# Rows of zeros for a small projection, and another order of Winograd products, in a four-layer network on one core

## The chip, the cores and the metric

The kernel runs on one core of one Trainium2 chip. The metric is the device time of one execution in microseconds, as the median over several executions. The profile comes from one further execution.

The engines are named as the profile names them: PE is the matrix engine (PEld its weight loads), DVE the vector engine, ACT the scalar engine with its activation functions, POOL the general-purpose engine, SP the engine that issues most of the DMAs. [...]

## The reference, cut to what matters

The input is a batch of three images of 256 channels and 48 x 48 points in float32. Four layers follow one another, each added to its input after a normalisation over groups of 8 channels:

```python
x = x + layer0(_gn(x))                                   # attention over 3 images, 1x1 convolutions
x = x + layer1(_gn(x), routing_ws, weight)               # 3x3 convolution, weights mixed per image
x = x + layer2(_gn(x), weight, bias)                     # plain 3x3 convolution with bias
x = x + layer3(_gn(x), ...)                              # state space layer (selective scan)

# layer 1: each image has its own weights, a mix of eight experts
routing = sigmoid(x.mean(axis=(2, 3)) @ routing_ws)
ws = einsum('ne,eoihw->noihw', routing, weight)

# layer 3, the part around the dt projection (DT_RANK = 16, D_STATE = 16, D_INNER = 512)
x_dbl = einsum('bld,ed->ble', u, x_proj_w)               # 48 values for each point: dt, B, C
dt = softplus(einsum('blr,dr->bld', x_dbl[..., :16], dt_proj_w) + dt_proj_b)
h = h * exp(dt * A) + dt * B * u                         # the scan, over the 2304 points of an image
```

## The kernel before, in words

**Stages.** Layer 0 runs until about 1500 us and takes nearly half of the time. The two convolutions run from about 1498 to 1995 us, the state space layer from about 1990 us to the end. Images are always taken in the order 2, 1, 0.

**The convolution stage.** A unit is one layer and one image: first image 2, 1 and 0 of layer 1, then the same three of layer 2. A unit has two halves of 24 rows (`h`), a half two output tiles of 128 channels (`m`). The 3 x 3 convolution is done in a Winograd form along the row: four points at a time are made from six products. `input_transform` (L316) normalises half an image into a padded tile `xpad` on ACT and makes the six input parts `vt[:, 0]` to `vt[:, 5]` of it with twelve DVE operations (L345 to L356). `output` (L642) calls `products` (L1630) once for each of the six taps: 6 float32 matmuls into a bank of PSUM, from a pool of five banks. Each matmul stands as two records in the profile. Taps 1 and 3 belong together, and 4 and 5: ACT copies the second of a pair to SBUF (L1650), DVE makes the sum and the difference (L1652, L1654), and these are put onto the four points of the image tile (L1659 to L1662). The outer taps 0 and 2 each go onto one point only, with a single DVE operation (L1664).

The order in `output` before the change is 1, 3, then 4, 5, then 0, 2:

```python
for i, j in ((1, 3), (4, 5)):
    pa, pb = products(u, vt, m, i), products(u, vt, m, j)
```

The input transform of a half is asked for one half ahead (`ahead = transformed(n + 1)`), so it stands in the program in front of the output tiles of the half before.

**The mixed weights.** During units 0 and 1 the weights of the next image are made (`mixed`, L265): 8 experts x 6 pieces of 384 KB come in by DMA on SP's queue (`part_of_kernel`, L251) into six buffers `wconv`. A piece is scaled on ACT for the first expert (L294) and added on DVE for the others (L296). With `shared=True` one piece of six is multiplied on PE instead (L282) and copied back by ACT (L290). After the last expert `kernel_transform` (L254) makes the six taps from the three kernel columns, for each half of the input channels six DVE operations: tap 4 and tap 5 (L259, L260), then tap 3 (L262) and, last, tap 1 (L263), which overwrites the middle column. Taps 0 and 2 are the outer columns as they are mixed. Thirteen steps of this are put behind each output tile. The plain weights of layer 2 are loaded and transformed during unit 2 (`plain`, L302).

The weights of image 2 and the input transform of the first half (`first_v`) are made at the end of layer 0. There the order on every engine is as written (`keep_order`, L2128); in the convolution stage it is left to the framework that builds the program, which takes what it reckons to be ready, earlier places in the program first.

**The state space stage.** It runs over 18 chunks (`todo`: three images, six chunks of 384 points each). A chunk has 8 steps of 8 scans (L1949) on DVE; their decays come from ACT (L1941) and their sums go through PE (L1971). The order is written out by hand in `plan` (L1432) and kept on all engines. In between, `project_u` (L1296) makes 96 rows: dt in rows 0 to 15, B in rows 32 to 47, C in rows 64 to 79, and zeros in the rows between. `take_dbc` (L1304) copies them into `dbc`, of 96 rows, and adds a column of the identity matrix, so that row 16 is all ones. `project_dt` (L1323) multiplies `dtsb`, which holds the dt projection's weights in rows 0 to 15 and its bias in row 16, by the first 17 rows of `dbc`; it is called twice a chunk, for two output tiles each (L1326). `keep_busy` (L1374) adds matmuls whose results nobody reads.

`dtsb` is a part of a block (L1138 to L1143) and is loaded once by `w3_loads` (L1153).

Of the kernel before, what the change touches and what calls it, by code (L numbers as in the profile page):

```python
# [12 lines left out]
ALU = mybir.AluOpType  # L13
# [3 lines left out]
P = 128  # L17
# [18 lines left out]
DI = 4  # L36
DS = 16
DTR = 16
# [46 lines left out]
def net(  # L85
# [230 lines left out]
    def input_transform(b, h, sc, sh):  # L316

        rows = HR + 2
        size = rows * PW
        t = pad.tile([P, 4, CT * size + 2], F32, name="xpad")  # L320

        nc.gpsimd.memset(t[:, :, 0 : CT * size + 1 : PW], 0.0)  # L322
        at = (0 if h == 0 else HR + 1) * PW
        for ct in range(CT):
            nc.gpsimd.memset(t[:, :, ct * size + at : ct * size + at + PW], 0.0)
        lo = 1 if h == 0 else 0
        first = h * HR - 1 + lo
        for ct in range(CT):
            src = xs[b][:, ct, :].rearrange("p (j r c) -> p j r c", j=4, c=TW)
            dst = t[:, :, ct * size : (ct + 1) * size].rearrange("p j (r c) -> p j r c", c=PW)  # L330
            nc.scalar.activation(
                dst[:, :, lo : lo + HR + 1, 1:], src[:, :, first : first + HR + 1, :],
                AF.Identity, bias=sh[:, ct : ct + 1], scale=sc[:, ct : ct + 1],
            )

        def column(j, at):
            return t[:, j, at : at + CT * size].rearrange("p (r c) -> p r c", c=PW)[:, :, :TW]

        d = [column(j, at) for j, at in ((3, 0), (0, 1), (1, 1), (2, 1), (3, 1), (0, 2))]
        vt = vp.tile([P, 6, CT, (HR + 2) * TW], F32, name="vt")  # L340
        o = [vt[:, i].rearrange("p t (r c) -> p (t r) c", c=TW) for i in range(6)]
        c = pad.tile([P, CT * rows, TW], F32, name="wc")
        e = pad.tile([P, CT * rows, TW], F32, name="we")
        tt, stt = nc.vector.tensor_tensor, nc.vector.scalar_tensor_tensor
        stt(c, d[2], -4.0, d[4], ALU.mult, ALU.add)  # L345
        stt(e, d[1], -4.0, d[3], ALU.mult, ALU.add)
        tt(o[1], c, e, ALU.add)
        tt(o[3], c, e, ALU.subtract)
        tt(c, d[4], d[2], ALU.subtract)
        tt(e, d[3], d[1], ALU.subtract)  # L350
        stt(o[4], e, 2.0, c, ALU.mult, ALU.add)
        stt(o[5], e, -2.0, c, ALU.mult, ALU.add)
        tt(o[0], d[0], d[2], ALU.subtract)
        stt(o[0], o[0], 4.0, c, ALU.mult, ALU.add)
        tt(o[2], d[5], d[3], ALU.subtract)
        stt(o[2], e, -4.0, o[2], ALU.mult, ALU.add)  # L356
        return vt

    def routing(b, psum, tag, stats):
# [23 lines left out]
    with ExitStack() as l0:  # L383
# [667 lines left out]
        i = NB - 1  # L1051
# [82 lines left out]
    def w3_rooms():  # L1134

        block = upools[0].tile([P, 6, 3, CT, 256], F32, name="u")
        block = block.rearrange("p a b c d -> p (a b c d)")
        w3v.update(divide(  # L1138
            block, ("w3sb", P, (NW3,)), ("winx", P, (CT, DI * P)), ("taps", P, (DI, DCONV, P)), ("convc", P, (DI * DCONV,)),
            ("amat", P, (DI * DS,)), ("rep", P, (4, 32)), ("less", P, (2, P)), ("zero", P, (8,)),  # L1140
            ("xn0", P, (CT, XH)), ("xn1", P, (CT, XH)), ("xi", P, (3, XH)),
            ("dtsb", DTR + 1, (DI * P,)),
        ))  # L1143
        rooms["xn"] = [w3v["xn0"], w3v["xn1"]]
        pieces = [wst.tile([P, 3 * 256], F32, name="wconv") for _ in range(6)]
        halves = [t.rearrange("p (t n) -> p t n", t=2) for t in pieces]
        for name, got in zip(("xg", "sq", "ot"), (halves[:2], halves[2:3], halves[3:5])):
            rooms[name] = got
        rooms["dbc"] = [halves[5][:96, j, :] for j in range(2)]
# [173 lines left out]
    def project_dt(k, m0):  # L1323
        for j in range(2):
            m = m0 + j
            nc.tensor.matmul(  # L1326
                bank[j], w3v["dtsb"][:, m * P : (m + 1) * P], k.dbc[: DTR + 1, :],
                start=True, stop=True,
            )

# [293 lines left out]
    with ExitStack() as l1:  # L1624
# [5 lines left out]
        def products(u, vt, m, i):  # L1630
            pc = ps.tile([P, 512], F32, tag="c", name="ps_c")
            for ct in range(CT):
                for dy in range(3):
                    nc.tensor.matmul(  # L1634
                        pc[:, :HN], u[:, i, dy, ct, m * P : (m + 1) * P],
                        vt[:, i, ct, dy * TW : dy * TW + HN],
                        start=ct == 0 and dy == 0, stop=ct == CT - 1 and dy == 2,
                    )
            between()
            return pc[:, :HN]  # L1640

        def output(b, h, m, u, vt, bias):

            xj = xs[b][:, m, :].rearrange("p (j n) -> p j n", j=4)[:, :, h * HN : (h + 1) * HN]
            tt, stt = nc.vector.tensor_tensor, nc.vector.scalar_tensor_tensor
            sums = []
            for i, j in ((1, 3), (4, 5)):
                pa, pb = products(u, vt, m, i), products(u, vt, m, j)
                cb = tmp.tile([P, HN], F32, name="cb")
                nc.scalar.copy(cb, pb)  # L1650
                add = tmp.tile([P, HN], F32, name=f"add{i}")
                tt(add, pa, cb, ALU.add)  # L1652
                sub = tmp.tile([P, HN], F32, name=f"sub{i}")
                tt(sub, pa, cb, ALU.subtract)  # L1654
                sums += [add, sub]
            p, q, r, s = sums
            for k, (minus, more, f) in enumerate(((p, r, 1.0), (q, s, 2.0), (p, r, 4.0), (q, s, 8.0))):
                if bias is None:
                    tt(xj[:, k], xj[:, k], minus, ALU.subtract)  # L1659
                else:  # L1660
                    stt(xj[:, k], xj[:, k], bias[:, m : m + 1], minus, ALU.add, ALU.subtract)
                stt(xj[:, k], more, f, xj[:, k], ALU.mult, ALU.add)  # L1662
            for i, k, f in ((0, 0, 1.5), (2, 3, 6.0)):
                stt(xj[:, k], products(u, vt, m, i), f, xj[:, k], ALU.mult, ALU.add)  # L1664


        units = [(layer, b) for layer in range(2) for b in ORDER]
# [506 lines left out]
def _layout(i):  # L2174
    l0 = {k[len("L0_conv_"):]: np.asarray(a) for k, a in i.items() if k.startswith("L0_conv_")}
    l3 = {k[len("L3_conv_"):]: np.asarray(a) for k, a in i.items() if k.startswith("L3_conv_")}
    cols = {k: _columns(l0[k]) for k, _ in VEC_WIDTHS if k in l0}
    cols["l2_bias"] = _columns(i["L2_conv_bias"])
    cols["norm_w"], cols["norm_b"] = _columns(l3["norm_w"]), _columns(l3["norm_b"])
    cols["conv_b"] = _columns(l3["conv_b"])  # L2180
    cols["D"] = _columns(l3["D_param"])

    cols["A_log"] = (
        l3["A_log"].reshape(DI, 4, 32, 4, 4).transpose(4, 2, 0, 3, 1).reshape(P, DI * DS)
    )
    vecs = np.concatenate([cols[k] for k, _ in VEC_WIDTHS], 1)

    w0 = {
        "cv1": _rows(l0["cv1_w"].T),
        "qkv": np.concatenate([_rows(a.T) for a in l0["qkv_w"]], 1),  # L2190
        "f1": np.concatenate([_rows(a.T) for a in l0["f1_w"]], 1),
        "f2": np.concatenate([_rows(a.T) for a in l0["f2_w"]], 1),
        "cv2": _rows(l0["cv2_w"].T),
    }

    xp = np.zeros((DI * P, 3, 32), np.float32)
    xp[:, :, :DS] = l3["x_proj_w"].T.reshape(DI * P, 3, DS)
    w3 = {
        "in": _rows(l3["in_proj_w"][DI * P :].T),
        "x": _rows(xp.reshape(DI * P, 96)),  # L2200
        "out": _rows(l3["out_proj_w"].T),
    }
    return {
        "x": np.asarray(i["x"]).reshape(B, CT * P, HN * 2, 4).swapaxes(2, 3).reshape(B, CT * P, N),
        "vecs": vecs,
        "w0": np.concatenate([w0[k] for k, _ in W0_WIDTHS], 1),

        "projw": l0["proj_w"].reshape(NB, P, HD, HEADS).transpose(0, 3, 2, 1).reshape(NB, P, P),
        "qkvb": l0["qkv_b"],
        "rw": np.asarray(i["L1_conv_routing_ws"]),  # L2210

        "we": np.asarray(i["L1_conv_weight"]).transpose(0, 2, 4, 3, 1).reshape(EXPERTS, 256, TAPS * 256),
        "w2": np.asarray(i["L2_conv_weight"]).transpose(1, 3, 2, 0).reshape(256, TAPS * 256),
        "w3": np.concatenate([w3[k] for k, _ in W3_WIDTHS], 1),
        "w3x": l3["in_proj_w"][: DI * P].T,
        "convw": l3["conv_w"].reshape(DI, P, DCONV).transpose(1, 0, 2).reshape(P, -1),
        "dtw": np.concatenate([l3["dt_proj_w"].T, l3["dt_proj_b"][None]]),
    }


# [17 lines left out]
```

## Time and profile before

| | |
|---|---|
| median of 3 runs | 3303.44 us (3302.32 to 3303.94) |
| the profiled execution | 3306.9 us, of which span 3305.1 us |
| mean granted PE clock | 0.983 of full speed |
| convolution stage | about 1498 to 1995 us |
| state space stage | about 1990 to 3305 us |

The span runs from the first to the last instruction of the profiled execution. In the lines of a timeline or of the chain, the first number is the time since the start of the span in us, the second a length in us; "x4" counts instructions, "17*128" gives the rows and columns of the array that a matmul uses, and a bracket the idle time before it and what ended it. In lines of waits, the three numbers are us in total, how many, and the longest.

### The profile page before, as it was taken

To read this page: it belongs to the slowest core of one execution; us is meant where nothing else is said; L and a number is where in the kernel's file an instruction comes from. 1 tells how busy PE (TensorE), PEld (TensorE's weight loads), DVE (VectorE), ACT (ScalarE), POOL (GpSimd) and SP (SyncE) were. 2 spreads that over 40 slices of the span, in tenths; PEclk is the share of its full clock that TensorE was granted. 3 is DMA by queue.
4 is the path that set the end of the run, shared out by engine and by line. 5 is a ranking of instruction groups with operands and counts; after the bars stand their busy time and mean duration, and the time that the engine had idled before them with its cause. 6 is when DMAs were issued, how large, how long until landed. Compare 5 with 4: busy or idle time off the path is not lost.

```text
span 3305.1 us, 54212 instructions
## 1 busy us (share of the span) xinstructions
PE 3140.9 (95%) x20918; PEld 1557.1 (47%) x20918; DVE 2867.9 (87%) x3225; ACT 2393.1 (72%) x3675; POOL 1338.7 (41%) x457
## 2 busy tenths in 40 slices
PE   7999999999999999998999998999999999999996
PEld 4334343363343434556677774444444444444442
DVE  3799989967988999389985449999999999999998
ACT  2688888848888888332223458888888888888885
POOL 0000000000000000120000008999999999999998
PEclk9999999999999999999999999999999999999998
DMA  4000000010000000484621025555555555555552
GB/s 168 32 8 10 7 10 6 8 48 5 8 7 8 8 7 9 153 313 165 222 80 42 34 75 132 139 129 128 136 130 142 140 138 130 130 134 137 141 132 69
DMA packets 182657, 290.98 MB, mean 88 GB/s; under 512 B 34850, under 2 KB 148962, under 8 KB 180467
## 3 DMA queue, kind: packets, MB, share of 16 engines
q1 hardware_dynamic: 169426, 268.53, 30.1%
q10 hardware_dynamic: 12960, 18.88, 1.7%
q8 instruction: 166, 2.72, 0.3%
q14 instruction: 105, 0.85, 0.1%
HBM read 236.24 MB, written 50.64 MB: 87 GB/s over the span
## 4 chain that ended last, share of the span: by engine, by line
PE 55%; DVE 28%; ACT 8%; issue 5%; DMA 2%; POOL 1%; SPq 0%; DVEq 0%; ACTq 0%; POOLq 0%
DVE hs L1949 19%; PE ps_s L640 16%; PE acc L653 15%; PE ps_c L1634 8%; DVE hs L1896 3%; ACT ps_da L1941 2%; PE ps_s L1035 2%; PE ps_y L464 2%; DVE u L296 2%; PE ps_m L667 2%; PE ps_m L713 1%; PE acc L531 1%; PE ps_g L1229 1%; PE ps_s L520 1%; DMA wconv<-in_we 1%
## 5 line engine op out<-in xcount | busy, mean ns | idle before, releaser
L644 ACT ACTIVATE pt<-ps_s 128x1024 f32<-128x1024 f32 x972 | 942.4, 1022 | 154.7 <-PE ps_s L640 142.2
L1949 DVE TENSOR_TENSOR_SCAN hs<-ps_da,hs 128x385 f32<-128x385 f32 x1152 | 1002.6, 936 | 5.6 <-ACT ps_da L1941 4.5
L859 DVE TENSOR_TENSOR part<-part,pt 128x2048 f32<-128x2048 f32 x396 | 906.7, 2290 | 41.2 <-ACT pt L644 18.4
L1941 ACT ACTIVATE ps_da<-dtr,u 128x384 f32<-128x384 f32 x1136 | 642.0, 580 | 116.2 <-DVE hs L1949 105.5
L164 POOL TENSOR_TENSOR rstd<-ve,mhalf 128x2 f32<-128x2 f32 (+1 forms) x25 | 16.0, 642 | 1440.6 <-DVE ve L162 1440.6
L640 PE MATMUL ps_s<-q,kt 32*128 32x512 f32 (+1 forms) x4320 | 576.4, 592 | 0.1
L653 PE MATMUL acc<-pt,vt 128*32 128x512 f32 (+1 forms) x4320 | 520.9, 561 | 0.2
L1634 PE MATMUL ps_c<-vt,u 128*128 128x288 f32 x1728 | 431.9, 410 | 17.6 <-DVE u L263 9.0
L1957 POOL TENSOR_TENSOR hc<-hs,x 128x3072 f32<-128x3072 f32 x72 | 405.3, 5629 | 11.2 <-DVE hs L1949 6.7
L1957 POOL TENSOR_TENSOR hc<-hs,bc 128x3072 f32<-128x3072 f32 x71 | 400.2, 5636 | 9.8 <-POOL hs L1915 3.9
L1634 PEld LDWEIGHTS ps_c<-vt,u 128*128 128x128 f32 x1728 | 330.0, 192 | 114.3 <-DVE u L263 9.7
L640 PEld LDWEIGHTS ps_s<-q,kt 32*128 32x128 f32 x4320 | 195.2, 183 | 199.1 <-issue 120.2
L653 PEld LDWEIGHTS acc<-pt,vt 128*32 128x32 f32 x4320 | 94.4, 108 | 353.4 <-issue 326.7
L1971 PE MATMUL ps_y<-hc,u 128*32 128x384 f32 x2304 | 226.9, 514 | 2.9 <-POOL hc L1957 2.9
L1915 POOL TENSOR_TENSOR hs<-dtur,bc 128x1536 f32<-128x1536 f32 x72 | 209.8, 2913 | 0.0
L1280 PE MATMUL ps_g<-u 128*128 128x384 f32 x576 | 193.6, 488 | 11.6 <-ACT u L1276 11.6
L1915 POOL TENSOR_TENSOR hs<-dtur,x 128x1536 f32<-128x1536 f32 x70 | 203.5, 2907 | 0.0
L1280 PEld LDWEIGHTS ps_g<-u 128*128 128x128 f32 x576 | 107.5, 189 | 94.2 <-ACT u L1276 22.5
L1971 PEld LDWEIGHTS ps_y<-hc,u 128*32 128x32 f32 x2304 | 62.2, 112 | 144.0 <-issue 128.7
L1650 ACT COPY cb<-ps_c 128x288 f32<-128x288 f32 x48 | 19.2, 399 | 150.7 <-PE ps_c L1634 141.5
L322 POOL MEMSET xpad<- 128x212 f32 x12 | 5.7, 475 | 291.6 <-ACT xpad L1685 221.5
L1399 PE MATMUL ps_g<-u 128*128 128x384 f32 x288 | 106.6, 503 | 13.1 <-ACT sz L1407 7.7
(295 smaller groups left out, 4169.8 us busy)
## 6 DMA issues: line engine op xcount, KB each, us to landing
wconv<-in_we SPq DMA_DIRECT2D x144, 384.0 KB, 4.6
dtr<-dtd SPq DMA_DIRECT2D x284, 192.0 KB, 3.7
dtur<-dtud SPq DMA_DIRECT2D x284, 96.0 KB, 4.2
wconv<-xd SPq DMA_DIRECT2D x36, 384.0 KB, 4.0
x<-bcd SPq DMA_DIRECT2D x72, 192.0 KB, 4.9
dtd<-x SPq DMA_DIRECT2D x36, 384.0 KB, 3.0
bc<-bcd SPq DMA_DIRECT2D x72, 192.0 KB, 5.0
dtuq<-dtud SPq DMA_DIRECT2D x284, 48.0 KB, 2.0
```

Source lines behind the costliest of these rows:

```text
L640: nc.tensor.matmul(s[:, j, cols], kt[r, mt * P : (mt + 1) * P], q[r, :n], start=True, stop=True,)
L644: nc.scalar.activation(p[:, h0 : h0 + 2, :], s, AF.Exp)
L653: nc.tensor.matmul(acc[h * HD : (h + 1) * HD, :n], vt[:, mt, g * P + h * HD : g * P + (h + 1) * HD], p[:, h, cols], start=mt == 0, stop=mt ...
L859: ): nc.vector.tensor_tensor(part, first, p, ALU.add)
L1280: nc.tensor.matmul(bank[m % 2], w3v["taps"][:, m, tap, :], w3v["xi"][:, m % 3, tap : tap + CH], start=tap == 0, stop=tap == DCONV - 1,)
L1399: nc.tensor.matmul(bank[j], w("in", ct * 512 + m * P, P), k.xn[:, ct, DCONV - 1 :], start=ct == 0, stop=ct == CT - 1,)
L1634: nc.tensor.matmul(pc[:, :HN], u[:, i, dy, ct, m * P : (m + 1) * P], vt[:, i, ct, dy * TW : dy * TW + HN], start=ct == 0 and dy == 0, stop ...
L1915: nc.gpsimd.tensor_tensor(states(s)[:, :, 2:4, 1:], chunks[at].rows[m][1].unsqueeze(1).broadcast_to([P, 2, 2, CH]), b_rows(s, 0, 2), ALU.mult,
L1941: nc.scalar.activation(slots[n % 3][:, 1 : CH + 1], chunks[at].rows[m][0][:, q, :], AF.Exp, scale=amat[:, col : col + 1],)
L1949: nc.vector.tensor_tensor_scan(b, slots[(8 * s + part) % 3][:, : CH + 1], b, 0.0, ALU.mult, ALU.add)
L1957: nc.gpsimd.tensor_tensor(hc, tiles[s][:, :, :, 1:], cb.broadcast_to([P, 2, 4, CH]), ALU.mult)
L1971: nc.tensor.matmul(k.y_ps[32 * q : 32 * q + 32, :CH], fold, hc[:, g, q, :], start=False, stop=g == 1 and q in ends,)
```

## The change

Two edits are made together.

1. `dtsb` gets 96 rows in place of 17. The host appends 79 rows of zeros to the weights, and `project_dt` multiplies by all of `dbc`. The result is the same sum with 79 more terms of zero.
2. In the first output tile (`m == 0`) of the first half (`h == 0`) of each image, `output` takes the outer taps first: 0, 2, then the pair 4, 5, then the pair 1, 3. Their accumulations (L1664) are put first as well (`ends`). `input_transform` makes its parts in the same order where `h == 0`: parts 0 and 2, then 4 and 5, then 1 and 3. All other output tiles and halves stay in the old order (in the second halves the parts come as 1, 3, 4, 5, 0, 2, as before).

```diff
         ...
+        def odd():
+            stt(c, d[2], -4.0, d[4], ALU.mult, ALU.add)
+            stt(e, d[1], -4.0, d[3], ALU.mult, ALU.add)
+            tt(o[1], c, e, ALU.add)
+            tt(o[3], c, e, ALU.subtract)
+
+        def outer():
+            tt(o[0], d[0], d[2], ALU.subtract)
+            stt(o[0], o[0], 4.0, c, ALU.mult, ALU.add)
+            tt(o[2], d[5], d[3], ALU.subtract)
+            stt(o[2], e, -4.0, o[2], ALU.mult, ALU.add)
+
         ...
-        stt(c, d[2], -4.0, d[4], ALU.mult, ALU.add)
-        stt(e, d[1], -4.0, d[3], ALU.mult, ALU.add)
-        tt(o[1], c, e, ALU.add)
-        tt(o[3], c, e, ALU.subtract)
+        if h:
+            odd()
         tt(c, d[4], d[2], ALU.subtract)
         tt(e, d[3], d[1], ALU.subtract)
+        if not h:
+            outer()
         stt(o[4], e, 2.0, c, ALU.mult, ALU.add)
         stt(o[5], e, -2.0, c, ALU.mult, ALU.add)
-        tt(o[0], d[0], d[2], ALU.subtract)
-        stt(o[0], o[0], 4.0, c, ALU.mult, ALU.add)
-        tt(o[2], d[5], d[3], ALU.subtract)
-        stt(o[2], e, -4.0, o[2], ALU.mult, ALU.add)
+        if h:
+            outer()
+        else:
+            odd()
         return vt
         ...
-            ("dtsb", DTR + 1, (DI * P,)),
+            ("dtsb", 96, (DI * P,)),
         ...
-                bank[j], w3v["dtsb"][:, m * P : (m + 1) * P], k.dbc[: DTR + 1, :],
+                bank[j], w3v["dtsb"][:, m * P : (m + 1) * P], k.dbc,
         ...
+            def ends():
+                for i, k, f in ((0, 0, 1.5), (2, 3, 6.0)):
+                    stt(xj[:, k], products(u, vt, m, i), f, xj[:, k], ALU.mult, ALU.add)
+
+            first = h == 0 and m == 0
+            if first:
+                ends()
             sums = []
-            for i, j in ((1, 3), (4, 5)):
+            for i, j in ((4, 5), (1, 3)) if first else ((1, 3), (4, 5)):
                 pa, pb = products(u, vt, m, i), products(u, vt, m, j)
         ...
-            p, q, r, s = sums
+            p, q, r, s = sums[2:] + sums[:2] if first else sums
         ...
-            for i, k, f in ((0, 0, 1.5), (2, 3, 6.0)):
-                stt(xj[:, k], products(u, vt, m, i), f, xj[:, k], ALU.mult, ALU.add)
+            if not first:
+                ends()
         ...
-        "dtw": np.concatenate([l3["dt_proj_w"].T, l3["dt_proj_b"][None]]),
+        "dtw": np.concatenate(
+            [l3["dt_proj_w"].T, l3["dt_proj_b"][None], np.zeros((95 - DTR, DI * P), np.float32)]
+        ),
```

## The prediction

> **What bounds the kernel now.** I read the page first (shares, granted clock), then the chain of waits in order of time, then the stretches, waits and timelines of the two places that the edits touch.
>
> ```profile
> PE 3140.9 (95%) x20918; PEld 1557.1 (47%) x20918; DVE 2867.9 (87%) x3225; ACT 2393.1 (72%) x3675; POOL 1338.7 (41%) x457
> ```
>
> Nearly everything is busy, so an average says nothing: each edit is priced where it lies. The dt projection (L1326) is in the last stage, a loop over 18 chunks whose clockwork is the scan on DVE. The chain shows the same five scans once a chunk:
>
> ```profile
> 2072.89 4.33 DVE hs L1949 x5
> ...
> 2144.86 4.33 DVE hs L1949 x5
> ...
> 2217.73 4.33 DVE hs L1949 x5
> ...
> 2290.58 4.33 DVE hs L1949 x5
> ...
> 2362.56 4.33 DVE hs L1949 x5
> ```
>
> The distances are 71.97, 72.87, 72.85 and 71.98 us. Two chunks of the four are 0.89 us longer, with the same instructions. The PE timeline of the first long one says why; its last line is the same spot in a short chunk:
>
> ```profile
> 2192.51 1.55 PE L1326 MATMUL ps_g<-wconv,u 17*128 17x384 f32 x4 [0.89 <-ACT x L1389]
> 2193.99 0.91 PE L1964 MATMUL ps_y<-x,diag 128*128 128x384 f32 x2
> 2194.83 2.47 PE L1971 MATMUL ps_y<-hc,u 128*32 128x384 f32 x16
> 2197.23 2.23 PE L1355 MATMUL ps_g<-dtu,ident 128*128 128x384 f32 x4
> ...
> 2340.57 1.50 PE L1971 MATMUL ps_y<-hc,u 128*32 128x384 f32 x16
> ```
>
> The same 16 matmuls take 2.47 us instead of 1.50. The stretches of L1326 (columns: length, PE busy and count, PEld busy and count, granted clock, DMA) show a halved clock for one stretch of 3.41 us:
>
> ```profile
> 2191.80:2195.21 3.41, 1.55 (x4) 0.66 (x4) 1.00 0.68 200
> 2195.21:2198.63 3.42, 0.00 (x0) 0.00 (x0) 0.50 0.67 175
> ...
> 2335.16:2338.57 3.41, 0.32 (x1) 0.29 (x2) 1.00 1.09 212
> 2338.57:2341.99 3.42, 1.23 (x4) 0.37 (x2) 1.00 1.02 292
> ```
>
> The clock drops after a stretch that holds all four 17-row matmuls, and stays after one that holds one of them. The other long chunks repeat it (half clock from 2266.9, 2628.7, 2700.4, 3062.2 and 3133.9): six of them.
>
> The second place is the convolution stage, where the mixed weights of the next image are made on DVE (L296, then L258 to L263) while PE multiplies. Stretches of its first two units (PE, PEld, DVE, ACT, POOL busy, granted clock), then PE's waits and DVE's:
>
> ```profile
> 1498.10:1584.60 86.50, 85.08 (x332) 62.89 (x332) 82.65 (x147) 19.96 (x32) 2.59 (x7) 0.98 0.54 189
> 1584.60:1591.80 7.20, 0.01 (x1) 0.01 (x1) 7.17 (x10) 7.20 (x11) 0.69 (x3) 0.71 0.51 198
> 1591.80:1684.80 93.00, 91.15 (x352) 68.39 (x352) 84.94 (x138) 23.75 (x36) 2.09 (x7) 0.97 0.63 212
> ...
> 1686.00:1758.00 72.00, 72.00 (x299) 56.53 (x300) 52.22 (x113) 19.80 (x26) 2.19 (x8) 1.00 0.07 26
> ```
>
> ```profile
> PE ps_c L1634 <- DVE u L263: 9.0, 2, 7.2
> ```
>
> ```profile
> DVE u L296 <- DMA wconv<-in_we: 6.7, 8, 1.2
> DVE wconv L258 <- ACT u L290: 2.3, 1, 2.3
> DVE add L1652 <- ACT cb L1650: 1.1, 1, 1.1
> ```
>
> PE waits 7.2 us at the change of image, for the last operation of the weight transform (L263 makes tap 1, which is multiplied first). But DVE never rests there (7.17 of 7.20), and from 1498 to 1685 it is idle for 11.9 us alone (the lengths less the DVE column). DVE bounds these two units; from 1686 on PE does (72.00 of 72.00).
>
> **Part 1, zero rows.** No instruction is added or removed. 36 calls of two matmuls (144 records of L1326) read 96 rows in place of 17. Their price is the nearest row's: L1355, 128 rows and the same 384 columns, takes 486 ns against 481, its weight load 190 against 184. That is at most 144 x 5 ns = 0.7 us, in gaps that PE has (0.89 us ahead of L1326): 0. The load of `dtsb` (L1153) grows from 34 to 192 KB; it stays one issue (0.34 us) on SP's queue, and the 512 KB load behind it took 7.0 us to land. First use is at 1954.7, 205 us after the issue at 1749.7: 0. If that cover went, it would cost some 2 us.
>
> The gain is the clock. [...] in the stretch 2191.80 to 2195.21 PE was busy for 2.70 us and lost the clock, in 2335.16 to 2338.57 for 1.93 us and kept it. So what is counted is not busy time. [...] I side with the trace: six drops x 0.89 = 5.3 us off. Bounds: 0 if zeros do not count, 6.2 if another execution meets seven drops.
>
> **Part 2, order of the products.** No instruction is added or removed either; six of the 24 output tiles take products 0, 2, 4, 5, 1, 3 in place of 1, 3, 4, 5, 0, 2, and six input transforms are made in that order. No DMA is moved. Four places:
>
> 1. First unit. PE starts at 1498.09, after the third operation of the input transform. Product 0 needs the fourth, 0.72 us later; half of that is lost, as the clock is halved there until 1502.3: +0.4 (0 to +0.7).
> 2. Change to the second image. Product 0 needs mixed weights only (done at 1583.7), so the 7.2 us wait goes, and the half clock behind it. But L263 is only no longer late for PE; DVE still has it, and an input transform of 8.6 us, ahead of its first use of a product. DVE was free at 1606.10 and started L1652 at 1607.16: -1.1, all that DVE can give back.
> 3. The weight pieces have six buffers; those that PE multiplies (L282) are held until PE comes to them (1612.35), and behind them SP's queue stops. DVE then waits 2.0 us for pieces between 1614.9 and 1622.5, and 2.2 more at 1658 to 1662. PE comes some 7 us sooner: -1.5 (0 to -4.1), most of the first group.
> 4. Change to the third image. PE waits 1.85 and 1.10 us, and starts the second output tile at 1696.22, 0.12 us after L1654 gave a PSUM bank free (1696.10). Product 0 is released by one operation, not two: -0.35. If its accumulation lands in DVE's hole of 2.35 us before L258, PE runs through from 1674.9: six products of 2.91 us end at 1692.4, -3.5 after a short wait for L290. I take -2.0; the order on DVE is not written by hand here, so either can come.
>
> Sum +0.4 - 1.1 - 1.5 - 2.0 = -4.2 us (+0.7 to -8.7). In the three units behind, PE never waits, so nothing is won or lost and the lead passes to the last stage: the chain goes through PE's L1634 and L1326 until 1969.
>
> **The sum.** -5.3 - 4.2 = -9.5. The profiled execution took 3306.9 us (span 3305.1 and 1.8 around it): 3297.4. It stands 3.5 above the median of the runs, 3303.4, which gives 3293.9.
>
> **The rivals.**
> - *Only the clock pays.* DVE has no slack, so PE's 7.2 us lead is eaten at the next PSUM bank. For: DVE's 84.94 of 93.00. Against: L1652 and L296 do wait for what PE does late. -5.0: 3298.4.
> - *The padding does nothing*, [...] because zeros do not count. Then -4.2 alone: 3299.2. [...]
> - *Slower: the two accumulations of products 0 and 2 (L1664) are queued on DVE ahead of the weight transform (L258 to L263).* They wait for PE, which ends product 2 near 1590.1, while DVE could work from 1583.6: 6.5 us per change of image, 13 for two. With 5.3 won it ends near 3311. It decides if such a wait passes some 4 us per change. Against: those operations come earlier in the program than L1664, and the order in the trace keeps that.
>
> **How the numbers follow.** Both parts work: 0.68, only the clock 0.17, the padding does nothing 0.08, slower 0.07. About 6.6 us (0.2%) is what a measurement of this kernel can tell from no change. Both parts together pass it unless part 2 gives under 1.3 (one in ten of these cases counts as same); the two rivals below it mostly do not. Faster 0.67, same 0.26, slower 0.07. Range: from 5.3 + 8.7 with a little more clock (3288.5) to the clock alone with the first unit's loss, and the padding alone (3300).
>
> **What would show it.** After: chunk distances all near 71.95, granted clock 1.00 from 2035 on but for the last 90 us, L1326 as 96*128. No wait of L1634 for L263 near 1584; PE's first L1634 of the second unit some 7 us sooner, but DVE's L1652 about 1 us; fewer waits of L296. I am wrong if the clock still halves after L1326, or if DVE waits on PE at L1664 ahead of L258.

## The result and the profile after

| | before | after |
| --- | --- | --- |
| median of six runs each | 3303.69 us (3299.53 to 3304.06) | 3289.18 us (3286.98 to 3290.58) |
| ratio of after to before, 95% interval | | 0.9957 [0.9947, 0.9968] |
| profiled execution, its span | 3306.9, 3305.1 us | 3289.2, 3287.5 us |
| mean granted clock of TensorE | 0.983 | 0.989 |

The change saves 14.5 us by the medians, 0.43%. The forecast was 9.5 (3293.9 for the median); the result lies inside its range of 3288.5 to 3300, near the low end.

In the profiled executions the spans differ by 17.6 us. I cut each span at four places that both traces share: the end of layer 0's last matmul, the last product of the convolutions (of layer 2; L1634 before, L1646 after), the first scan of chunk 0 and the first scan of chunk 17.

| stretch (us) | before | after | difference |
| --- | --- | --- | --- |
| span's start to layer 0's last matmul | 1490.66 | 1487.64 | -3.02 |
| from there to the convolutions' last product | 504.63 | 495.10 | -9.53 |
| chunk 0's first scan to chunk 17's | 1230.32 | 1224.77 | -5.55 |
| the rest (the two joints and the last chunk) | 79.47 | 79.99 | +0.52 |

The first row is not the change's: layer 0 runs the same code, and over the fourteen kernels traced for this study (twelve experiments, before and after) its end lies anywhere from 1481.87 to 1490.66. The profiled execution of before sits at the late end of that. The second row belongs to the order of products (8.9 of its 9.5 us lie within layer 1, 258.5 to 249.6) and the third to the zero rows: 15.1 together, beside 14.5 by the medians.

**The scan stage.** The chain of waits of after, in order of time (start, length, what), shows the same eight matmuls once a chunk:

```profile
2043.89 2.86 PE ps_g L1241 x8
...
2115.86 2.86 PE ps_g L1241 x8
...
2187.81 2.86 PE ps_g L1241 x8
...
2259.77 2.86 PE ps_g L1241 x8
...
2331.72 2.86 PE ps_g L1241 x8
```

The distances are 71.97, 71.95, 71.96 and 71.95 us; the 72.87 of before is gone. The six stretches at half clock between 2040 and 3200 us have become none. These are the stretches from 2040 to 3200 us of before and of after (length; busy time and count of PE, PEld, DVE, ACT, POOL; granted clock; DMA share; GB/s):

```profile
2040.00:3200.00 1160.00, 1095.54 (x5180) 547.85 (x5180) 1146.68 (x1365) 1016.91 (x2021) 1139.63 (x324) 0.99 0.56 135
2040.00:3200.00 1160.00, 1086.74 (x5188) 548.69 (x5186) 1151.24 (x1373) 1019.17 (x2026) 1145.05 (x326) 1.00 0.56 136
```

The records of L1338 (L1326 before; nanoseconds, lowest, median and highest) show that the rows cost next to nothing on PE, 486 ns against 481:

```profile
L1338 PE MATMUL ps_g<-wconv,u x144: 483/486/592, 1942.8 to 3188.2; 96*128 96x384 f32 x144
```

**Layer 1, where weights are mixed beside the products.** First the stretches from each image's first product to the next image's, for the three images of layer 1, of after and then of before (columns as above):

```profile
1495.95:1583.22 87.27, 84.94 (x330) 63.26 (x331) 81.37 (x146) 19.42 (x30) 2.58 (x7) 0.97 0.53 184
1583.22:1664.60 81.38, 79.91 (x322) 60.24 (x320) 79.69 (x134) 24.54 (x38) 2.08 (x7) 1.00 0.66 229
1664.60:1737.08 72.48, 71.97 (x297) 55.92 (x296) 61.37 (x115) 19.97 (x27) 2.08 (x7) 1.00 0.11 36
```

```profile
1498.09:1591.79 93.70, 85.10 (x333) 62.91 (x333) 89.83 (x157) 27.15 (x42) 3.28 (x10) 0.96 0.54 190
1591.79:1677.28 85.49, 83.64 (x322) 62.80 (x322) 79.77 (x132) 16.41 (x26) 1.39 (x4) 0.96 0.64 215
1677.28:1749.04 71.76, 70.65 (x292) 55.17 (x293) 54.52 (x106) 19.23 (x27) 2.10 (x7) 1.00 0.06 19
```

Compare the DVE columns. The same work is cut elsewhere. When the second image's first product starts, DVE of after has done 8.5 us less (81.37 against 89.83). In the second image it does as much as before in 4.1 us less, because its idle time falls from 5.7 us to 1.7. In the third image it does 6.9 us more (61.37 against 54.52). There it had 17 us to spare, so the debt is paid where DVE limits nothing.

The timeline of PE at the change to the second image, before and then after (start, length, operation, idle time before it in brackets):

```profile
1577.72 3.56 PE L1634 MATMUL ps_c<-vt,u 128*128 128x288 f32 x14
1581.12 2.99 PE L282 MATMUL ps_g<-wconv,each 128*128 128x384 f32 x8
1584.20 0.38 PE L186 MATMUL ps_gm<-mv,gmat 128*128 128x2 f32 x2
1591.79 8.60 PE L1634 MATMUL ps_c<-vt,u 128*128 128x288 f32 x22 [7.20 <-DVE u L263]
```

```profile
1576.76 4.04 PE L1646 MATMUL ps_c<-vt,u 128*128 128x288 f32 x16
1580.64 2.74 PE L282 MATMUL ps_g<-wconv,each 128*128 128x384 f32 x8
1583.22 9.14 PE L1646 MATMUL ps_c<-vt,u 128*128 128x288 f32 x37
```

From the start of the first image's last product to the second image's first PE took 13.6 us before (1578.21 to 1591.79) and 5.5 after (1577.73 to 1583.22). In before, a half clock from 1587.6 to 1597.9 then stretched the first product from 2.91 us to 5.92. In after the clock stays at 1.00 over the same time. Together 11.1 us. The stretch in before and in after:

```profile
1587.64:1597.88 10.24, 6.09 (x13) 4.33 (x14) 10.24 (x14) 7.05 (x8) 0.69 (x3) 0.50 0.60 205
1587.64:1597.88 10.24, 10.24 (x44) 8.04 (x43) 10.24 (x14) 7.74 (x10) 0.70 (x3) 1.00 0.60 195
```

PE's waits of after between 1480 and 1740 (line, releaser: us in all, times, longest), the whole list, and then the two longest of DVE's:

```profile
PE ps_c L1646 <- DVE vt L350: 8.3, 1, 8.3
PE ps_g L282 <- DMA wconv<-in_we: 3.8, 4, 2.0
PE ps_c L1646 <- ACT cb L1669: 0.4, 1, 0.4
```

```profile
DVE add L1671 <- ACT cb L1669: 8.2, 2, 5.2
DVE u L296 <- DMA wconv<-in_we: 4.8, 7, 1.4
```

No wait for L263 is left. What is late now: PE stands 3.8 us for weight pieces ahead of L282 (1.3 before, all of it in the first image). DVE's 8.2 us at L1671 fall in the third image, where it has time.

### The profile page after: what moved, and what is told of

Read it like the earlier page. It is cut to its first block, busy times and chain, and to the rows that moved or that the text cites. A ratio compares the mean times of both kernels' runs of the same rounds, so it can differ in the third digit from the quotient of the medians.

```text
span 3287.5 us, 54212 instructions
## 1 busy us (share of the span) xinstructions
PE 3123.5 (95%) x20918; PEld 1554.6 (47%) x20918; DVE 2866.2 (87%) x3225; ACT 2392.3 (73%) x3675; POOL 1338.5 (41%) x457
## 4 chain that ended last, share of the span: by engine, by line
PE 55%; DVE 29%; ACT 8%; issue 5%; DMA 2%; POOL 1%; SPq 0%; DVEq 0%; ACTq 0%; POOLq 0%
DVE hs L1968 19%; PE ps_s L652 16%; PE acc L665 15%; PE ps_c L1646 9%; DVE hs L1915 3%; ACT ps_da L1960 3%; PE ps_y L476 2%; PE ps_g L1241 2%; PE ps_m L679 2%; PE ps_m L725 1%; DVE u L296 1%; PE ps_s L1047 1%; PE acc L543 1%; PE ps_s L532 1%; DMA wconv<-in_we 1%
## 5 line engine op out<-in xcount | busy, mean ns | idle before, releaser
L871 DVE TENSOR_TENSOR part<-part,pt 128x2048 f32<-128x2048 f32 x396 | 906.4, 2289 | 41.3 <-ACT pt L656 18.5
L1646 PE MATMUL ps_c<-vt,u 128*128 128x288 f32 x1728 | 429.8, 409 | 8.7 <-DVE vt L350 8.3
L1646 PEld LDWEIGHTS ps_c<-vt,u 128*128 128x128 f32 x1728 | 328.9, 191 | 104.1 <-issue 9.1
L1990 PE MATMUL ps_y<-hc,u 128*32 128x384 f32 x2304 | 219.6, 500 | 3.1 <-POOL hc L1976 3.1
L1669 ACT COPY cb<-ps_c 128x288 f32<-128x288 f32 x48 | 19.2, 401 | 138.8 <-PE ps_c L1646 128.6
```

What stands on the lines that cost most here:

```text
L871: ): nc.vector.tensor_tensor(part, first, p, ALU.add)
L1646: nc.tensor.matmul(pc[:, :HN], u[:, i, dy, ct, m * P : (m + 1) * P], vt[:, i, ct, dy * TW : dy * TW + HN], start=ct == 0 and dy == 0, stop ...
L1990: nc.tensor.matmul(k.y_ps[32 * q : 32 * q + 32, :CH], fold, hc[:, g, q, :], start=False, stop=g == 1 and q in ends,)
```

## Experiments

In the table, *wait* is PE's idle time between layer 0's last matmul and the first product, *conv* the time from layer 0's last matmul to the last product of the convolutions (layers 1 and 2), *halved* the number of stretches of half clock that start between 2040 and 3200 us. All are from one profiled execution each. *Time* is the median of the runs, *ratio* that to before with its interval. Where no ratio stands, there was one run. Before was measured again beside each group of experiments: 3303.2 (e1 to e4), 3304.2 (e5 to e8) and 3303.9 us (e9 to e12).

| kernel | wait | conv | halved | time, us | ratio |
| --- | --- | --- | --- | --- | --- |
| before | 7.4 | 504.6 | 6 | 3303.7 | |
| after | 8.3 | 495.1 | 0 | 3289.2 | 0.9957 [0.9947, 0.9968] |
| e1, 96 rows only | 6.4 | 504.4 | 0 | 3298.8 | 0.9989 [0.9982, 0.9995] |
| e2, order only | 6.9 | 493.4 | 5 | 3289.3 | 0.9959 [0.9945, 0.9972] |
| e3, 32 rows | 6.1 | 503.5 | 4 | 3303.9 | |
| e4, spare matmuls | 6.3 | 504.0 | 13 | 3341.9 | |
| e5, products' order only | 13.0 | 498.9 | 5 | 3299.1 | 0.9987 [0.9980, 0.9994] |
| e6, parts' order only | 13.7 | 510.4 | 4 | 3311.3 | 1.0026 [1.0017, 1.0035] |
| e7, tap 1 third | 6.9 | 498.3 | 0 | 3291.3 | 0.9965 [0.9953, 0.9976] |
| e8, two images only | 7.4 | 495.0 | 0 | 3289.1 | 0.9954 [0.9940, 0.9968] |
| e9, 96 rows in the second call only | 7.6 | 503.8 | 1 | 3299.8 | |
| e10, 64 rows | 6.2 | 503.6 | 0 | 3296.5 | |
| e11, late accumulations | 8.3 | 497.8 | 0 | 3291.0 | 0.9960 [0.9947, 0.9974] |
| e12, e5 again | 12.9 | 499.0 | 5 | 3298.7 | |

**e1 and e2: each part alone.** e1 is before with the zero rows:

```diff
+ROWS = 96
         ...
-            ("dtsb", DTR + 1, (DI * P,)),
+            ("dtsb", ROWS, (DI * P,)),
         ...
-                bank[j], w3v["dtsb"][:, m * P : (m + 1) * P], k.dbc[: DTR + 1, :],
+                bank[j], w3v["dtsb"][:, m * P : (m + 1) * P], k.dbc[:ROWS, :],
         ...
```

(the host appends the zeros, as in after.) e2 is after with these lines as before (17 rows).

> Zero rows alone, the old order of products. [...] the six halved stretches of the scan stage go and nothing else moves: 5.3 us under before (4.5 to 6.2), chunk distances near 71.95 throughout. If the saving in the changed kernel came from something else (the two parts helping each other), 0 to 2 us.

> New order alone, 17 rows. Theory: the weight transform and the next input transform leave the loop that PE waits in, and what DVE has left of them is done in the third unit, where DVE has room; then 8 to 12 us under before, the second unit's first product some 8 us sooner, and the halved clock of the scan stage is still there, five to seven times. Rival (the prediction's own step): DVE bounds the first two units, so not more than 4 us, and the rest of what the changed kernel won was the earlier end of layer 0 in that one execution.

e1 takes the halved stretches from 6 to 0, shortens the scan stage from 1230.32 to 1225.03 us (-5.3), leaves the convolutions at 504.4, and is 4.4 us faster by the medians. e2 shortens the convolutions by 11.3 us, keeps five halved stretches, and is 13.8 faster, where 8 to 12 were expected. So the parts do what they were priced for, each in its own stage. The medians do not add up exactly: 4.4 + 13.8 = 18.2 against 14.5 for both. The intervals allow it (after: 10.6 to 17.5; e1: 1.7 to 5.9). In the traces e2 is 2.0 us longer than after: its scan stage is 5.1 longer, its layer 0 0.8, its convolutions 1.7 and the rest 0.5 shorter. Why the median of e2's five runs came out as low as after's was not settled.

**e3, e10, e9: how many rows, and where.** e3 and e10 are e1 with 32 and 64 rows. In e9 only the second of a chunk's two calls reads 96:

```diff
         ...
+        rows = ROWS if m0 else DTR + 1
         ...
-                bank[j], w3v["dtsb"][:, m * P : (m + 1) * P], k.dbc[: DTR + 1, :],
+                bank[j], w3v["dtsb"][:rows, m * P : (m + 1) * P], k.dbc[:rows, :],
         ...
```

> Zero rows to 32 only. [...] the clock still halves five to seven times in the scan stage, and the time is that of before. [...] if the padding helps in another way, some or all of the halvings go.

> The kernel of before with zero rows to 64. [...] none or one halved stretch between 2040 and 3200 us. If the count went by busy time alone[...], 4 to 6 would stay as with 17 and 32 rows (6 and 4 in the profiled executions).

> The kernel of before with 96 rows of weights, but only project_dt(k, 2) reads them all; project_dt(k, 0), some 11 us earlier in a chunk, goes on with 17 rows. Theory ([...] only the stretch with project_dt(k, 2) falls short): no halved stretch between 2040 and 3200 us, the 17 chunk distances all 71.85 to 72.0, the scan stage from first to last chunk 1149.7 to 1150.3 us as with 96 rows in both calls, some 5 less than before. Rival (any of the two calls with few rows can fall short, or the gain comes from something else that the zero rows bring): 4 to 6 halved stretches stay, scan stage 1153 to 1155.5.

Four halved stretches stay with 32 rows (five to seven were expected) and none is seen with 64. In e3 the clock was halved behind four 32-row matmuls as it was behind the 17-row ones of before; this is e3's PE timeline around the start of its halved stretch, at 2480.2 (L1972 takes 2.50 us in place of 1.50):

```profile
2477.47 1.55 PE L1327 MATMUL ps_g<-wconv,u 32*128 32x384 f32 x4 [0.89 <-ACT x L1390]
2478.96 0.91 PE L1965 MATMUL ps_y<-x,diag 128*128 128x384 f32 x2
2479.80 2.50 PE L1972 MATMUL ps_y<-hc,u 128*32 128x384 f32 x16
```

e9 was to have none and has one, at 2540.0. Its stretches there, and PE's timeline:

```profile
2536.60:2540.00 3.40, 2.98 (x17) 1.79 (x20) 3.40 (x5) 3.30 (x9) 3.40 (x3) 0.99 0.22 72
2540.00:2543.40 3.40, 3.40 (x20) 0.94 (x12) 3.40 (x6) 3.25 (x9) 3.40 (x2) 0.50 0.75 197
```

```profile
2536.81 1.16 PE L1379 MATMUL ps_r<-hs,ident 128*128 128x128 f32 x8 [0.17 <-DVE hs L1951]
2538.21 1.55 PE L1328 MATMUL ps_g<-wconv,u 17*128 17x384 f32 x4 [0.24 <-ACT wconv L1308]
2539.69 2.59 PE L1973 MATMUL ps_y<-hc,u 128*32 128x384 f32 x16
```

This is the first call, still with 17 rows, and the drop comes 41.3 us after the chunk's first scan, where those of before come 51.7 to 52.9 after it. PE was busy for 2.98 of 3.40 us and lost the clock all the same. So the statement "only the stretch with project_dt(k, 2) falls short" was wrong: here a drop follows the first. e2's drop at 2096.9 is another, 41.0 us after its chunk's first scan. Each of these two made its chunk 0.5 us longer, where one behind the second call costs 0.9. With both calls at 64 or 96 rows no trace had a halved stretch between 2040 and 3200 us (e10; after, e1, e7, e8, e11), so padding both calls is right.

Busy time does not order these stretches. Beside e9's, with 2.98 of 3.40 us, here is one of before that kept its clock with PE busy for 1.93 of 3.41:

```profile
2335.16:2338.57 3.41, 1.93 (x6) 0.97 (x6) 3.41 (x6) 3.00 (x7) 3.41 (x2) 1.00 1.09 212
```

What does decide was not shown. What the runs show is a count, in one trace each: 6 halved stretches with 17 rows (before), 4 with 32 (e3), 1 with 17 and 96 (e9), none with 64 (e10) or 96 (e1).

**e4: spare work in place of rows.** 17 rows, and four 128x128 identity matmuls behind the second call, in each chunk:

```diff
         (11, PE_, 1, lambda k: project_dt(k, 2)),
+        (11, PE_, 1, lambda k: keep_busy(ident, 4)),
```

> 17 rows as before, and four matmuls (ident by ident, 128 columns, nobody reads them) on PE behind the second dt projection of each chunk. If it is the counted work that the stretch lacks, this repairs the clock as the zero rows do: chunk distances near 71.95, about 5 us under before. If the row count of the dt projection itself matters, the halvings stay, and the spare matmuls cost up to 1 us a chunk where PE has no gap.

It is 38 us slower, and the clock is halved 13 times: more than either of the two expectations allowed. The PE timeline ahead of the drop at 2124.4 shows what the spare matmuls do:

```profile
2121.25 1.55 PE L1326 MATMUL ps_g<-wconv,u 17*128 17x384 f32 x4 [0.89 <-ACT x L1389]
2123.74 1.49 PE L1377 MATMUL ps_r<-ident 128*128 128x128 f32 x8 [0.93 <-DVE hs L1897]
2125.02 1.49 PE L1965 MATMUL ps_y<-u,diag 128*128 128x384 f32 x2
```

The spare matmuls write a tile that DVE still reads, so they wait 0.93 us for L1897, and L1965 starts behind them, at 2125.02. In the 3.40 us ahead of the drop PE was busy for 2.21 us, where before had 2.70 of 3.41 ahead of its drop at 2195.21; no chunk is shorter than 73.1 us. This experiment does not test whether work by itself keeps the clock. It shows what filling matmuls cost here, where their output tile has another reader: PE waits 19.7 us for L1897 between 2040 and 3200 us (32 times), where it waited 1.8 for the same line (L1896) in before. More rows in a matmul that must run anyway need no tile.

**e5, e12 and e6: the halves of the new order.** e5 takes products 0 and 2 first but makes the input parts in the order of before; e6 makes the outer parts first but multiplies in the order 1, 3, 4, 5, 0, 2. Both have 17 rows. e12 is e5 once more.

```diff
 e5, e12: output() as in after, input_transform() as in before
 e6:      input_transform() as in after, output() as in before
```

> Old parts order in the input transform, new order of the products, 17 rows. Theory: what counts is which weights PE asks for first, so nearly all of the order's gain is here: within 2 us of the kernel with the order alone. At the very first unit PE must then wait for part 0, which comes last but three in the old order: some 4 us later there. Rival: the parts must come in the same order, or the gain is gone (over 5 us lost).

> New parts order in the input transform, old order of the products, 17 rows. Both theories: no gain, and at the first unit product 1 waits for the ninth operation or later in place of the third, some 5 us. So 0 to 6 us over before.

> A second look at products 0 and 2 first with the parts in the order of before and 17 rows, whose profiled execution (3293.6 us) was the fastest of its 20. If the mixing of layer 1 differs from run to run in this form: unit 0's first product to unit 3's in 242 to 247 us, where the first look had 239.7 and before 251.0. If it does not: 239 to 241 again, and the spread comes from the work ahead of layer 1 and from the clock.

PE's first waits in e12, and then in e6:

```profile
PE ps_c L1634 <- DVE vt L354: 12.9, 1, 12.9
```

```profile
PE ps_c L1646 <- POOL xpad L325: 13.7, 1, 13.7
PE ps_c L1646 <- DVE u L263: 7.1, 2, 4.6
```

The order of products alone gives the whole gain behind the first product: in e12 the three images of layer 1 take 84.0, 85.6 and 70.3 us, 239.9 in all, against 251.0 before and 241.1 after. But product 0 is then the first to be wanted and its input part nearly the last to be made, so PE stands 5.5 us longer ahead of it than in before: the convolutions are 5.6 us shorter in e12, and the time 5.1 by the medians of e5. The forecast for e5, within 2 us of the order alone, missed: the convolutions are 5.5 us longer than in e2, the median 9.8. The order of parts alone only makes the first product later (13.7, as parts 1 and 3 now come last; the list names POOL's xpad, but in DVE's timeline L345, which makes part 1, runs from 1499.23 to 1500.04, and the product starts at 1500.30). It leaves the wait for L263: the convolutions are 5.7 us longer and the time 7.1 by the medians (3311.3 against 3304.2), somewhat over the 0 to 6 that were expected. So one half gives some 5 us, the other costs 7, and together they shorten the convolutions by 9.5 to 11.3.

The profiled executions of e5 and e12 differ by 5.2 us in span. Their convolutions are the same to 0.2 us; layer 0 ended at 1481.87 in one and at 1487.42 in the other. So the difference between these two comes from ahead of the change.

**e7: tap 1 third.** After, with the first tile's order 0, 2, 1, 3, 4, 5:

```diff
-            for i, j in ((4, 5), (1, 3)) if first else ((1, 3), (4, 5)):
+            for i, j in ((1, 3), (4, 5)):
         ...
-            p, q, r, s = sums[2:] + sums[:2] if first else sums
+            p, q, r, s = sums
```

> The changed kernel, but in the new tiles the pair 1, 3 comes ahead of the pair 4, 5: 0, 2, 1, 3, 4, 5. PE comes to tap 1 some 5.8 us after it starts, and L263 ends about 12 us after that start: it should wait some 6 us there. Theory (PE's time is what counts, DVE's leftover can wait): the kernel gets slower by 3 to 6 us against the changed one. Rival (DVE bounds these units and eats PE's lead): within 1 us of the changed kernel.

```profile
PE ps_c L1646 <- DVE u L263: 3.6, 2, 2.0
```

The wait for L263 comes back, 3.6 us in two places, and the convolutions lose 3.2 against after (498.3 to 495.1). Two products of 2.91 us do not cover the transform of 8 us; four do. By the medians it costs 2.1 us, less than the 3 to 6 that were expected, and the intervals of e7 and after overlap; the trace, not the time, shows the effect.

**e8: the new order in images 2 and 3 only.**

```diff
-            first = h == 0 and m == 0
+            first = h == 0 and m == 0 and at_unit in (1, 2)
```

(the input parts likewise.)

> The changed kernel with the new order only where weights are mixed beside the work, that is in the second and third unit; the first unit and the plain convolution keep the old order of parts and products. The first unit can then start after three DVE operations in place of four. Theory: 0.5 to 1 us under the changed kernel, or equal within what can be measured; the plain convolution's order is worth nothing. If the new order in the plain convolution or the first unit helps, over the changed kernel.

Convolutions of 495.0 us and a median of 3289.1, as after. The gain lies at the two changes of image under which weights are still being made. At the other first tiles no effect of the order can be measured.

**e11: accumulations late.** After, with products 0 and 2 first but their two accumulations at the end of the tile, so that two of five PSUM banks are held:

```diff
         ...
             if first:
-                ends()
+                for i in (0, 2):
+                    made[i] = products(u, vt, m, i)
         ...
-            if not first:
-                ends()
+            ends()
```

(`ends` takes what stands in `made`.)

> The kernel of after (order of input parts, products 0 and 2 first, 96 rows), but the two accumulations of those products stay at the end of the tile, as before; their two banks of five are held until then. Theory A (the gain is that the products no longer wait at a change of image, since 0 and 2 need only what is ready first): the change to the second image gains as in after, 8 to 12 us between the first products of units 0 and 3 against before; two banks held cost PE a wait for a bank in each first tile, some 1 to 3 us each; time 3289 to 3296. Theory B (the gain needs the accumulations early on DVE, so that banks come free while DVE puts its transform behind): most of the 10 us goes, 3296 to 3300.

```profile
1495.07:1582.35 87.28, 85.27 (x331) 63.61 (x331) 81.39 (x146) 19.31 (x30) 2.58 (x7) 0.96 0.53 183
```

The change to the second image is the same to 0.01 us (87.28 from first product to first product, after 87.27). The convolutions are 2.7 us longer (497.8), spread over the third, fourth and sixth unit. So theory A holds: the gain is PE's freedom to start, not an earlier release of banks. No version measured here beats after by more than the measurement tells.

## Why the prediction was right, and where its sizes were off

**Part 1, zero rows: -5.3 forecast, -5.55 in the trace of after, -5.3 in e1.** Six drops went, of 0.9 us each. That rows of zeros keep the clock here held: with 17 and 32 rows the drops are there (6 and 4), with 64 and 96 none. That PE pays next to nothing for the rows held too: 486 ns a record against 481. Why the rows keep the clock was not shown: the prediction's reason for it was its author's estimate. It allowed for a seventh drop, but for fewer than six only if zeros did nothing. Yet where the drops fall on a chunk (41.0 us after its first scan in e2's at 2096.9, 51.7 to 52.9 in before) and how many there are differs between executions. With 17 or 32 rows in both calls the traces (e4 aside) had 6, 5, 4, 5, 4 and 5 drops (before, e2, e3, e5, e6, e12). The scan stages of these six take 1228.5 to 1230.3 us, those with 96 rows in both calls some 1225 (e8 1226.6). So the part is worth some 3.5 to 5.5 us, not one number, and the six drops of before's trace were the most that any of them had.

**Part 2, order: -4.2 forecast, -9.5 in the trace of after.** This is the mis-sized term, and it lies outside its own bounds (+0.7 to -8.7). By its steps, measured from layer 0's last matmul:

| step | forecast | after | e2 | how, in after |
| --- | --- | --- | --- | --- |
| 1, first unit | +0.4 | +1.5 | +0.3 | product 0 starts 0.9 later and the half clock costs 0.6 more |
| (not foreseen) rest of the first unit | 0 | +1.0 | -0.5 | PE waits for weight pieces at L282, 2.0 at the longest |
| 2, change to the second image | -1.1 | -11.2 | -11.0 | 8.1 of waiting and 3.0 of half clock |
| 3, weight pieces within the second unit | -1.5 | +2.3 | +1.8 | two stops of PE for pieces, about 1.0 each; the rest small |
| 4, change to the third image | -2.0 | -2.6 | -2.1 | the waits for L263 and L262 (1.85 and 1.10) go, 0.4 for a copy comes |
| the units behind | 0 | -0.6 | +0.2 | |

Steps 2 to 4 agree between the two executions of this order. What differs is the first unit, by 2.7 us, and the units behind, by 0.8 the other way; so neither is a fixed cost of the order.

Step 2 failed in its last sentence: "-1.1, all that DVE can give back". What it said of DVE came true: its first output operation of the second image moved by only 0.8 us (1602.16 to 1601.37), 0.5 of which after was ahead already at the first image's last product. But PE does not need DVE at that moment. By 1601 it had run six products in after, on five PSUM banks; ACT's copy of product 5 (L1669, at 1595.06) had freed one without DVE. So PE kept the 11 us through step 2. DVE then lived on waits that it no longer had (idle 5.7 to 1.7 us in the second image) and carried 6.9 us of work into the third, where it had 17 us to spare. "DVE never rests there" was right and bounds DVE, not PE. The prediction should have asked by when DVE's work is needed, and whether a later stage has room for it.

Step 3 had the sign of PE's time wrong. In the second unit PE comes to its pieces 3 to 12 us sooner, while the transfers land at most 4.6 us sooner and some of them later; its waits for pieces there grow from none to 1.5 us. What DVE won in that unit (L296's waits for pieces, 4.0 to 1.2) is 2.8, but on DVE. In step 4 the prediction took the bank that L1654 gave free 0.12 us ahead of the second tile for what PE waits for. PE did not stand there in before: its products follow each other every 2.91 us. In after that tile's first product starts at 1684.37, 0.37 us late behind ACT's copy.

So the sum was right in part by luck. Part 1 held in size (-5.3 forecast, -5.55 measured), its reason was not shown. Part 2 gave more than twice its forecast, by a way that the prediction had ruled out, and the total stayed 0.7 us inside the range because the medians gave 14.5 us where the forecast's bounds reached 14.9.

**The rivals.** Only the clock pays: excluded by e2. Padding does nothing: excluded by e1's trace (no halved stretch, scan stage 5.3 us shorter). Slower, through L1664 queued ahead of the transform: in after its successor L1660 stands at 1601.37, behind L263 (1594.04), as the order in the program said.

## What to carry over

Where one engine waits for the last operation of another's chain, giving it first the work that needs only what is ready can pay the whole wait, although the other engine is saturated: compare the cover (here four products, 11.6 us, against 8 us of transform) and look for a later stage in which the debt fits. Order both ends: e5 and e6 show that consumer and producer reordered alone give -5 and +7 us, and together -14 (e2). Look for stretches of half clock even in a busy loop: here matmuls of 17 rows went with six of them in before's trace, the same matmuls at 96 rows with none, and zero rows at 5 ns a record were a cheaper filling than more matmuls, which waited 0.93 us for their output tile (e4). Price such a part from more than one trace: the kernels with 17 or 32 rows in both calls, other than e4, had four to six drops.

## What was not expected of the hardware

TensorE's clock was halved after a stretch in which PE was busy for 2.98 of 3.40 us (e9), and stayed full after one of before with 1.93 of 3.41. What sets the two apart was not shown. One halved stretch of 3.41 us cost the chunk 0.9 us behind the second call (before) and 0.5 behind the first (e2, e9). At the change of image, the wait cost more than its length: in before, 10.2 us at half clock came with 7.2 us of standing, and the first product took 3.0 us longer in them (5.92 against 2.91); in after, without the wait, the clock stayed at 1.00 over the same time.
